# A masked cross-attention with layer norm: the order of all five engines' work written anew

## The chip, the cores and the metric

The kernel runs on one core of one Trainium2 chip. TensorE (PE in the profile) multiplies into PSUM, VectorE (DVE) and ScalarE (ACT) read PSUM and SBUF, GpSimd (POOL) works on SBUF alone, and SyncE (SP) only issues DMAs. Each engine takes its instructions strictly in the order in which the program lists them, and engines wait for each other by semaphores. The metric is the device time of the kernel in microseconds (us): before the change 507.44, the median of 3 runs (507.23 to 507.62).

## The reference

```python
qs  = (q @ wq).reshape(Bq, Lq, H, HD)        # q = x: 4 x 2048 rows of 512; H = 16 heads of HD = 32
ks_ = (k @ wk); vs = (v @ wv)                # k = v = context: 4 x 77 rows of 512
scores = einsum('bhqd,bhkd->bhqk', qs, ks_) / sqrt(HD)
scores = where(mask, -inf, scores)
attn = einsum('bhqk,bhkd->bhqd', softmax(scores), vs)
out  = attn @ wo + q
mu, var = mean(out), mean((out - mu) ** 2)   # over the 512 columns
return (out - mu) / sqrt(var + 1e-5) * gamma + beta
```

Everything is float32. The kernel multiplies the large matrices as a high and a low part (a float32 number rounded to the format `F32R`, and the rest), and adds three products: high by high, high by low, low by high.

## The kernel before, in words

The 8192 rows of x are cut into 64 tiles of 128 rows; two tiles are a block (32 blocks, numbered b), and four tiles are a group of 512 rows whose q is computed together (16 groups). The work is a list of small steps, one letter each, and the table `ORDER` writes out by hand in which order all of them are recorded. Since every engine works in the order of recording, the table sets each engine's order as well. No scheduler moves anything later. The steps that matter here:

- `Q` (`q_visit`, `q_rows`, matmuls on L275): one quarter of the heads' q for a group: 12 matmuls of 128x512, for each of 4 chunks of the contraction x high by wq high, x low by wq high, x high by wq low. `q` (`q_evac`, L289) copies the result from PSUM to SBUF on DVE.
- `S` (`scores`, L405): the scores of one tile, 64 small matmuls into four PSUM banks. `T` (`maxima`, L422) on DVE adds the mask and finds a row's greatest score, a quarter of the heads a step; `e` (`exps`, L437) on ACT exponentiates and sums; `r` (L447, DVE) takes the reciprocal, `n` (L452, POOL) multiplies by it.
- `t` (L473, DVE) transposes a tile in 32x32 squares into a buffer `B`, and 12 steps `P` (L484) per block are the DMAs that regroup it into `PT`, each by a queue that its last letter names: s for SP, a for ACT, g for POOL.
- `V` (`av`, L498): the product with the values for one block, 32 recorded matmuls. `a` (L527, ACT) rounds it to the high part `AH`, `b` (L531, DVE) makes the low part `AL`.
- `O` (`o_proj`, L554): the output projection of one tile, 12 matmuls of 128x512 into a bank `po`: for each chunk AH by wo high, AH by wo low, AL by wo high. `+` (L563, DVE) adds x, `s` (L577, L578, DVE) takes mean and variance, `v` (`rsqrt`, L583 to L586, four small operations on POOL) makes scale and shift for a block, `k` (`scale`, L592, ACT) applies them, `f` and `)` (L595, L598, POOL) multiply by gamma and add beta, `w` (SP) stores.
- `g` (`load_xT`) and `x` (`load_x`) are loads by SP; `i` (L265, ACT) and `j` (L269, POOL) make the high and low parts of x.

On PE there are so three kinds of stretches: wide matmuls (Q, O and, early, the values and keys), scores (S), and values' products (V). A second table, `SLOTS`, says which buffer each new tile takes; PSUM has 8 banks. `wait_for` adds a wait by hand: where DVE makes the low part of a weight out of two SBUF tiles (`F`, `G`), the next POOL step of the kinds j, n, f and `)` waits until that is done. The last eight tiles (`u`, `y`, `z`, `~` steps, the set `ALONE`) are normalised one by one by other functions.

Of the kernel before, what the change touches and what calls it, by code (L numbers as in the profile page):

```python
# [17 lines left out]
P = 128  # L18
# [16 lines left out]
for b in range(4):  # L35
# [7 lines left out]
NPB = 3  # L43
KSCALE = 1.0 / HD**0.5
# [7 lines left out]
F2 n1 e2.2 g6 T3.3 T3.0 T3.2 T2.1 j4 t1 P0.3s P0.2s P0.0s P0.5s e3.3 Q6 q6 G0 q7 B0 B2 e2.0 G3 G1 D0 e2.1 q5 e3.2 T3.1  # L52
P0.9s e2.3 r2 e3.1 e3.0 i6 G2 g7 P0.10s P0.11s S4 T4.3 e4.3 P0.7s T4.2 P0.8s i7 e4.2 B1 r3 Z1.s T4.0 e4.0 n2 T4.1 t2
Z0.s Q10 P0.4s n3 t3 P0.6s D2 P0.1s Z3.s S6 T6.2 T6.0 j6 D1 T6.3 P1.3s q10 T6.1 e4.1 r4 P1.0s P1.5s Q9 q9 e6.0 S5 T5.2
T5.0 e6.1 P1.2s P1.1s P1.8s j7 Q14 Z16.s P1.6s n4 t4 S7 Z2.s T7.3 e5.2 e6.3 e6.2 e7.3 T7.0 e7.0 T7.2 T5.3 T5.1 r6
P1.11s T7.1 e7.1 e7.2 q14 P1.10s P1.9s P1.7s P1.4s Q8 q8 Q11 q11 r7 Q13 n6 t6 e5.3 e5.1 e5.0 S9 T9.0 n7 T9.3 t7 r5 n5
V1 a1.1 a1.0 b1.0 x0 g8 i8 j8 g9 b1.1 T9.1 V0 a0.1 T9.2 Z8.s b0.1 x3 Z15.s O2 L1 i9 x2 S8 P3.6s P3.2s P3.8s j9 t5 e9.1
a0.0 b0.0 e9.2 e9.0 +2 T8.3 e8.3 T8.1 e8.1 =24.8 T8.0 e8.0 s2 T8.2 O3 +3 s3 q13 v1 P3.10s Z14.s P3.0s O0 P3.7s P3.9s
P3.1s Z4.s P3.5s e9.3 S10 T10.2 +0 Y1 Z13.s P3.4s x4 T10.3 e8.2 P3.11s P2.7s P2.8s P3.3s T10.1 e10.3 r9 k3 e10.1 T10.0
# [115 lines left out]
def xattn_layernorm(  # L175
# [84 lines left out]
    def load_xT(g, c):  # L260
        fx[g, c] = buf([P, 2, GRP], F32, "xtf", name=f"xtf_{g}_{c}")
        nc.sync.dma_start(fx[g, c], xT[g, :, c : c + 2])
# [538 lines left out]
```

## Time and profile before

| | us |
|---|---|
| median of 3 runs | 507.44 (507.23 to 507.62) |
| profiled execution, first to last instruction (span) | 506.2 |
| median less span | 1.24 |
| PE busy | 498.8 (99%) |
| ACT busy | 473.9 (94%) |
| DVE busy | 460.5 (91%) |
| POOL busy | 421.3 (83%) |

For the profiled execution the profile gives the span; the time of that execution as the runs measure it is not listed, so the span stands for it. Busy time is the union of an engine's instructions; an instruction's recorded length can overlap the next one's, since the engines are pipelined. The granted TensorE clock was 0.998 over the span.

### The profile page before, as it was taken

The numbers are of one execution on the slowest core, as the hardware profiler recorded it, in microseconds if no ns is written. First come the engines' busy times: TensorE is split into PE (matmuls) and PEld (weight loads), VectorE is DVE, ScalarE is ACT, GpSimd is POOL, SyncE is SP. The second block draws the span as 40 slices with busy tenths as digits, with TensorE's granted clock in tenths as the row PEclk, the third lists the DMA queues.
The fourth block names the chain that finished last, engine by engine and source line by source line (L and its number), as shares of the span: only waits on it lengthen the run. The fifth ranks groups of instructions, "written<-read, shape, count | busy, mean of one in ns | idle before, by whom it ended". The sixth has DMA issues, their size and how long they took to land.

```text
span 506.2 us, 20312 instructions
## 1 busy us (share of the span) xinstructions
PE 498.8 (99%) x6831; PEld 383.1 (76%) x6831; DVE 460.5 (91%) x2539; ACT 473.9 (94%) x2248; POOL 421.3 (83%) x387
## 2 busy tenths in 40 slices
PE   9999999999999999999999999999999999999995
PEld 6987778777777777777777777777777777877773
DVE  5799988999899999898898898998999999899997
ACT  6699999999999999999999999999999998999851
POOL 2666464789886798989989887999998999999896
PEclk9999999999999999999999999999999999999999
DMA  8957577889886796859887778877888769888746
GB/s 306 396 197 175 135 212 183 221 210 217 247 242 178 177 248 199 249 165 253 243 216 204 200 207 240 230 201 193 248 232 225 207 177 293 247 199 222 183 150 232
DMA packets 58782, 110.86 MB, mean 219 GB/s; under 512 B 9462, under 2 KB 11278, under 8 KB 58678
## 3 DMA queue, kind: packets, MB, share of 16 engines
q1 hardware_dynamic: 54502, 101.30, 71.1%
q0 software_dynamic: 2496, 5.77, 4.0%
q10 hardware_dynamic: 1680, 2.49, 2.0%
q8 instruction: 54, 0.88, 0.8%
q14 instruction: 50, 0.41, 0.3%
HBM read 41.79 MB, written 16.78 MB: 116 GB/s over the span
## 4 chain that ended last, share of the span: by engine, by line
PE 98%; DMA 1%; DVE 1%; ACT 0%; issue 0%; DVEq 0%
PE po L554 36%; PE pq L275 35%; PE pa L498 11%; PE sc L405 11%; PE pv L326 2%; PE pk L299 1%; PE pq L685 1%; DMA stage_a<-kin 1%; PE pa L513 0%; DVE xtl L637 0%; PE po L543 0%; DVE st L606 0%; DVE po L634 0%; ACT woh L672 0%; DVE mvt L608 0%
## 5 line engine op out<-in xcount | busy, mean ns | idle before, releaser
L437 ACT ACTIVATE pbuf<-pbuf,nm 128x77 f32<-128x77 f32 x1024 | 353.0, 358 | 5.2 <-DVE nm L422 3.6
L437 ACT ACTIVATION_READ_ACCUMULATOR pbuf<-pbuf,nm 128x1 f32 x1024 | 203.2, 198 | 0.0
L422 DVE CUSTOM_DVE_ANT_0 pbuf<-sc,mb 128x77 f32<-128x77 f32 x1024 | 169.7, 231 | 7.4 <-PE sc L405 5.8
L452 POOL TENSOR_TENSOR pbuf<-pbuf,ri 128x1232 f32<-128x1232 f32 x63 | 142.2, 2258 | 36.7 <-DVE ri L447 25.4
L554 PE MATMUL po<-woh,AH 128*128 128x512 f32 x256 | 103.5, 404 | 0.0
L473 DVE STREAM_TRANSPOSE B<-pbuf 128x1280 f32<-128x1280 f32 x64 | 96.1, 1502 | 5.8 <-POOL pbuf L452 2.4
L275 PE MATMUL pq<-xth,wqh 128*128 128x512 f32 (+1 forms) x256 | 100.8, 394 | 0.2
L554 PE MATMUL po<-wol,AH 128*128 128x512 f32 x256 | 99.9, 390 | 0.0
L554 PE MATMUL po<-woh,AL 128*128 128x512 f32 x256 | 99.8, 390 | 0.0
L275 PE MATMUL pq<-xth,wql 128*128 128x512 f32 (+1 forms) x256 | 98.1, 383 | 0.0
L275 PE MATMUL pq<-xtl,wqh 128*128 128x512 f32 (+1 forms) x256 | 98.1, 383 | 0.0
L422 DVE DVE_READ_ACCUMULATOR2_ANT nm<- 128x1 f32 x1024 | 84.4, 82 | 0.0
L598 POOL TENSOR_TENSOR o<-o,bet 128x512 f32<-128x512 f32 x56 | 72.1, 1291 | 1.8
L595 POOL TENSOR_TENSOR o<-o,gam 128x512 f32<-128x512 f32 x56 | 72.2, 1293 | 0.1
L269 POOL TENSOR_TENSOR xtl<-xtf,xth 128x1024 fp32r<-128x1024 f32 x28 | 67.2, 2404 | 3.9 <-ACT xth L265 3.2
L405 PEld LDWEIGHTS sc<-kct,q 32*64 32x64 f32 x4096 | 51.4, 130 | 22.6 <-issue 12.2
L405 PE MATMUL sc<-kct,q 32*64 32x77 f32 x4096 | 61.2, 238 | 0.0
L498 PE MATMUL pa<-PT,vsb 96*32 96x256 f32 x992 | 59.7, 382 | 0.0
L554 PEld LDWEIGHTS po<-woh,AH 128*128 128x128 f32 x256 | 48.0, 188 | 14.3 <-issue 2.5
L275 PEld LDWEIGHTS pq<-xth,wqh 128*128 128x128 f32 x256 | 48.1, 188 | 13.7 <-DVE nm L422 1.2
L554 PEld LDWEIGHTS po<-woh,AL 128*128 128x128 f32 x256 | 48.1, 188 | 10.5 <-DVE AL L531 0.2
L275 PEld LDWEIGHTS pq<-xth,wql 128*128 128x128 f32 x256 | 48.1, 188 | 9.7
(108 smaller groups left out, 638.6 us busy)
## 6 DMA issues: line engine op xcount, KB each, us to landing
PT<-B SPq DMA_DIRECT2D x330, 128.0 KB
xtf<-xT SPq DMA_DIRECT2D x28, 512.0 KB
o<-x SPq DMA_DIRECT2D x56, 256.0 KB
out<-o SPq DMA_DIRECT2D x56, 256.0 KB
PT<-B POOLq DMA_DIRECT2D x25, 128.0 KB, 4.0
PT<-B ACTq DMA_DIRECT2D x17, 128.0 KB
stage_a<-kin SPq DMA_DIRECT2D x4, 410.0 KB
xtf<-xT SPq DMA_DIRECT2D x4, 256.0 KB
```

The source lines that it names most:

```text
L269: return nc.gpsimd.tensor_tensor(l[:, c : c + 2], fx.pop((g, c)), xh[g][:, c : c + 2].bitcast(F32), ALU.subtract)
L275: nc.tensor.matmul(pq, w[:, c, m * P : (m + 1) * P], r[g][:, c, rs], start=(n == 0), stop=(n == 11))
L326: nc.tensor.matmul(pv[: rows.stop - rows.start], ctx_s[c][i][:, rows], v[c], start=(n == 0), stop=(n == 11))
L405: mm = nc.tensor.matmul(sc[j][r0 : r0 + SR, g * NK : (g + 1) * NK], qs[q, g, rs.start + r0 : rs.start + r0 + SR], kct[q, g, t // TPB, keys ...
L422: nc.vector.tensor_tensor_reduce(pb[:, h // 2, (h % 2) * NK : (h % 2 + 1) * NK], scs[t][j][:, g * NK : (g + 1) * NK], mb[:, t % TPB, keys_ ...
L437: nc.scalar.activation(pb[:, h // 2, (h % 2) * NK : (h % 2 + 1) * NK], pb[:, h // 2, (h % 2) * NK : (h % 2 + 1) * NK], AF.Exp, bias=nmax[t ...
L452: return nc.gpsimd.tensor_tensor(pv, pv, rv.to_broadcast((P, NP, 2, NK)), ALU.mult)
L473: nc.vector.transpose(bt.rearrange("p c q r -> p q c r"), pbuf[t % NPB].rearrange("p q (c r) -> p q c r", c=5),)
L498: nc.tensor.matmul(pas[b, g // 2][HD * j : HD * (j + 1), (g % 2) * BLK : (g % 2 + 1) * BLK], vsb[:, 2 * b // TPB, h % 2, HD * (h // 2) : H ...
L554: nc.tensor.matmul(pos[t], a[:, c, rs], w[:, c, :], start=(first and c == 0 and n == 0), stop=(c == NC_D - 1 and n == 2),)
L595: return nc.gpsimd.tensor_tensor(od[t], od[t], gam, ALU.mult)
L598: return nc.gpsimd.tensor_tensor(od[t], od[t], bet, ALU.add)
```

## The change

The table `ORDER` is replaced from its second line on, and `SLOTS` with it. Every step of before is there once, on the same operands, with these differences.

- **Kinds on PE.** Counted in the table from before and in the new one, the number of places where PE goes from one kind (wide, scores, values) to another falls from 151 to 135 (the description of the change counts 134). Stretches of wide visits fall from 58 to 45, runs of scores from 62 to 60 (S46 S47 and S60 S61 are new pairs), runs of values' products by one (V28 V29). A V is now followed at once by an S in 26 places (15 before), and by a wide visit in 3 (15 before).
- **Low parts last.** In Q and O the 8 matmuls with the high parts stand first, the 4 with the low part last.
- **Scaling on VectorE.** 37 of 56 tiles are scaled by DVE (`k….1`, a subtraction and multiplication with two per-row scalars) and 19 by ACT as before. Where both tiles of a block are, two of POOL's four small operations in `v` fall away. The next POOL step of the kinds j, n, f, `)` or v waits until the scaling is done.
- **q on ScalarE.** 28 of the 60 copies of q go from DVE to ACT.
- **Queues.** ACT's queue issues 101 of the regrouping DMAs (21 before; the description counts the 97 of whole blocks), POOL's 9 (31 before), SP's 286 (344 before). ACT's queue also issues 20 loads of x and 8 of x transposed. In all ACT issues 129 DMAs, 108 more than before.
- **Pauses in PE's queue.** A number behind an O or Q spreads that many NOPs among the visit's matmuls: 147 in all, 19 of them in 9 visits early in the kernel, the rest in 15 visits from O48 on.

```diff
-T1.1 Q4 T1.2 e0.3 F0 T1.3 I0 e1.2 r0 n0 S2 q4 e1.0 S3 T2.3 T2.0 Q7 N Y0 x1 Q5 i5 F1 e1.1 F3 R2 e1.3 j5 i4 t0 T2.2 r1
+T1.1 Q4.4 T1.2 e0.3 F0 T1.3 I0 e1.2 r0 n0 S2 q4 e1.0 S3 T2.3 T2.0 Q7.4 N Y0 x1 Q5 i5 F1 e1.1 F3 R2 e1.3 j5 i4 t0 T2.2
...
+def hi_then_lo(wh, wl, hi, lo):
+    return [(w, hi, c) for c in range(NC_D) for w in (wh, wl)] + [(wh, lo, c) for c in range(NC_D)]
...
+CENTRED = {int(w[1:].split(".")[0]) for w in ORDER.split() if w[0] == "k" and "." in w}
...
-        nc.sync.dma_start(fx[g, c], xT[g, :, c : c + 2])
+        (nc.scalar if by_scalar else nc.sync).dma_start(fx[g, c], xT[g, :, c : c + 2])
...
+    def pad(n, nops):
+        for _ in range((n + 1) * nops // 12 - n * nops // 12):
+            nc.tensor.nop(hint="pad")
...
-        for c in range(NC_D):
-            for w, r in ((wqh, xh), (wqh, xl), (wql, xh)):
-                nc.tensor.matmul(pq, w[:, c, m * P : (m + 1) * P], r[g][:, c, rs], start=(n == 0), stop=(n == 11))
-                n += 1
+        for w, r, c in hi_then_lo(wqh, wql, xh, xl):
+            nc.tensor.matmul(pq, w[:, c, m * P : (m + 1) * P], r[g][:, c, rs], start=(n == 0), stop=(n == 11))
+            pad(n, nops)
+            n += 1
...
-            nc.vector.tensor_copy(once(qd, g, [P, NG, GRP], F32, "q")[:, m, :], pq)
+            copy = nc.scalar.copy if by_scalar else nc.vector.tensor_copy
+            copy(once(qd, g, [P, NG, GRP], F32, "q")[:, m, :], pq)
...
-        nc.sync.dma_start(od[t], x[t * P : (t + 1) * P, :])
+        (nc.scalar if by_scalar else nc.sync).dma_start(od[t], x[t * P : (t + 1) * P, :])
...
+        for n, (w, a, c) in enumerate(hi_then_lo(woh, wol, ah, al)):
+            nc.tensor.matmul(pos[t], a[:, c, rs], w[:, c, :], start=(first and n == 0), stop=(n == 11))
+            pad(n, nops)
...
-        nc.gpsimd.tensor_tensor(rn[:, 1, :], mv[:, :, 0], rn[:, 0, :], ALU.mult)
-        nc.gpsimd.tensor_tensor(rn[:, 1, :], rn[:, 1, :], mneg, ALU.mult)
+        if not {2 * b, 2 * b + 1} <= CENTRED:
+            nc.gpsimd.tensor_tensor(rn[:, 1, :], mv[:, :, 0], rn[:, 0, :], ALU.mult)
+            nc.gpsimd.tensor_tensor(rn[:, 1, :], rn[:, 1, :], mneg, ALU.mult)
...
+        if t in CENTRED:
+            mean = mvs[t // 2][:, tt, 0:1]
+            return nc.vector.tensor_scalar(o, pos.pop(t, o), mean, rn[:, 0, tt : tt + 1], ALU.subtract, ALU.mult)
...
-            if op in "FG":
+            if op in "FG" or op == "k" and k and int(k) in CENTRED - IN_PSUM:
                 shared = ins
-            elif shared and op in "jnf)":
-                wait_for(ins, shared, "VectorE's pass over two tiles of SBUF is begun ahead of GpSimd's")
+            elif shared and op in "jnf)v":
+                wait_for(ins, shared, "VectorE's pass over both of its ports is begun ahead of GpSimd's")
```

In the changed kernel's file the steps stand some 15 lines lower (scores L420, values' product L513, maxima L437, exponentials L452, transposes L488, regroupings L499, scaling L607 on DVE and L608 on ACT).

**PE, around the values' product of block 2.** `sc` are score banks, `pa` the values' product, `pq` a bank of q; a number is a buffer's. Before:

```order
L405 MATMUL sc_2_1864<-kct,q_1140 64x77
L405 MATMUL sc_3_1865<-kct,q_1140 64x77
L498 MATMUL pa_0_1916<-PT_1538,vsb 32x256 x8
L498 MATMUL pa_1_1917<-PT_1538,vsb 32x256 x8
L275 MATMUL pq_3_1957<-xth_1281,wqh 128x512
L275 MATMUL pq_3_1957<-xtl_1283,wqh 128x512
L275 MATMUL pq_3_1957<-xth_1281,wql 128x512
```

And now:

```order
L420 MATMUL sc_2_1853<-kct,q_1155 64x77
L420 MATMUL sc_3_1854<-kct,q_1155 64x77
L513 MATMUL pa_0_1912<-PT_1416,vsb 32x256 x8
L513 MATMUL pa_1_1913<-PT_1416,vsb 32x256 x8
L420 MATMUL sc_0_1986<-kct,q_1155 64x77
L420 MATMUL sc_1_1987<-kct,q_1155 64x77
L420 MATMUL sc_2_1988<-kct,q_1155 64x77
```

The wide visits that stood between the values' product and the next tile's scores are gone from there; they stand together with others, ahead of and behind this place.

**PE, the end of a visit of q** (`xth` and `xtl` are the high and low parts of x, `wqh` and `wql` those of wq), now:

```order
L288 MATMUL pq_0_1823<-xth_1303,wqh 128x512
L288 MATMUL pq_0_1823<-xth_1303,wql 128x512
L288 MATMUL pq_0_1823<-xtl_1422,wqh 128x512 x4
L420 MATMUL sc_0_1851<-kct,q_1155 64x77
L420 MATMUL sc_1_1852<-kct,q_1155 64x77
```

Before, the low part came with the second matmul of a visit, as the first fence's last three rows show; now it comes with the ninth.

**ACT, some tiles after the first blocks.** Rows of `o` are scalings, `pbuf` exponentials (x4 is a quarter of the heads), `AH` a high part. Before:

```order
L527 CAST AH_2993<-pa_0_2975 128x512
L437 ACTIVATE pbuf_80,sum_3027<-pbuf_80,nm_2960 128x77 x4
L265 CAST xth_2833<-xtf_2_2653 128x1024
L437 ACTIVATE pbuf_82,sum_2907<-pbuf_82,nm_2801 128x77 x4
L592 ACTIVATE o_2862<-o_2862,rn_2915 128x512
L592 ACTIVATE o_2354<-o_2354,rn_2915 128x512
```

And now:

```order
L554 DMA o_3115<-x 128x512
L452 ACTIVATE pbuf_80,sum_3034<-pbuf_80,nm_3006 128x77 x8
L499 DMA PT_3085<-B_3003 32x2x512
L452 ACTIVATE pbuf_80,sum_3034<-pbuf_80,nm_3006 128x77 x4
L499 DMA PT_3085<-B_3003 32x2x512
L452 ACTIVATE pbuf_81,sum_3187<-pbuf_81,nm_3103 128x77 x4
L272 DMA xtf_2_3192<-xT 128x1024
```

Where two scalings stood among the exponentials, loads of x and regrouping DMAs now stand between their groups; before, no DMA stood on this queue ahead of block 23's.

More of the change, by code (lines that the diff above doesn't have):

```diff
@@ L55 @@
[L55 to L59, printed above, removed]
@@ L126 @@
-x48 e56.3 w45 e56.2 r56 v23 k46 P26.11s P26.10g T57.3 V25 P26.9a P26.2a w41 x57 x63 x53 e57.0 n55 t55 P27.5s S58
-P27.6s T58.2 a25.0 e57.3 e57.2 e57.1 n56 P27.9s P27.8g T58.0 a25.1 e58.0 f46 P27.1g )46 Q60 k47 P27.0s w46 x50 x60 q60
-b25.0 P27.11g r57 n57 T58.3 T58.1 e58.1 e58.2 t56 e58.3 Q62 S59 T59.3 s49 T59.1 T59.2 q62 P27.10g x62 e59.3 P27.4a O48
-+48 r58 s48 b25.1 f47 P27.3g T59.0 P27.2g t57 P27.7a Q61 q61 )47 w47 e59.2 Q63 q63 v24 k48 k49 V26 a26.0 b26.0 n58
-P28.4g x52 P28.0s S60 T60.3 T60.1 P28.10g x51 x55 P28.5s P28.1s T60.2 f49 P28.6g P28.3g P28.2g e59.0 e59.1 r59 n59 f48
@@ new lines @@
+S59 t56 x57.1 f47 s49 T59.2 r57 T59.1 e58.0 P27.9s v24 Q63.11 Q60.10 P27.11s e58.1 k49.1 a26.0 T59.3 e59.1 n57 T59.0
+x50.1 e59.0 b26.1 w45 x63.1 r58 t57 O50.19 q63.1 q60.1 P28.5s e59.3 b26.0 n58 e59.2 f49 S60 t58 k48.1 P28.11s P28.1s
++50 T60.0 e60.0 S61 P28.4s )49 T60.1 T60.2 )47 )46 w47 O51.13 r59 s50 w49 P28.8s P28.6s P28.9a T60.3 T61.1 T61.0 e60.1
+T61.3 n59 V27 P28.3a S62 +51 P28.0s e60.2 t59 x53 e60.3 O52.9 T61.2 f48 P28.10a s51 x52 P28.7s P28.2s T62.3 r60 T62.1
+e61.3 a27.1 O53.4 a27.0 x56 b27.1 v25 b27.0 x54.1 e61.2 P29.7a P29.9s P29.2s P29.0s e62.3 P29.11a e61.1 T62.2 +53
@@ L146 @@
+IN_PSUM = {int(w[1:].split(".")[0]) for w in ORDER.split() if w[0] == "k" and w.endswith(".2")}
 SLOTS = {
     "mm": (
[L148 to L151 removed]
@@ L153 @@
+        "1042673536741053265031472650314275065213764051430672156730"
     ),
@@ L156 @@
     "xtl": "10101010101010101",
-    "xtf": "010101010101010110101010101010",
-    "PT": "10100101010101010101010101010101011",
+    "xtf": "010101010101001000101010101011",
+    "PT": "1010010101010101010101010101010101",
     "B": "0101011010101010101010101010101010",
@@ L543, in resid, with o_proj @@
         nc.tensor.matmul(pos[t], ident, od[t], start=True, stop=False)
-    def o_proj(t):
+    def o_proj(t, nops=0):
         b, tt = divmod(t, 2)
@@ L551, in o_proj @@
             pos[t] = bank(f"po_{t}")
-        for c in range(NC_D):
-            for n, (a, w) in enumerate(((ah, woh), (ah, wol), (al, woh))):
-                nc.tensor.matmul(
-                    pos[t],
-                    a[:, c, rs],
-                    w[:, c, :],
-                    start=(first and c == 0 and n == 0),
-                    stop=(c == NC_D - 1 and n == 2),
-                )
+        for n, (w, a, c) in enumerate(hi_then_lo(woh, wol, ah, al)):
+            nc.tensor.matmul(pos[t], a[:, c, rs], w[:, c, :], start=(first and n == 0), stop=(n == 11))
+            pad(n, nops)
     def residual(t):
+        if t in IN_PSUM:
+            return residual_psum(t)
         nc.vector.tensor_tensor(od[t], pos.pop(t), od[t], ALU.add)
```

207 lines of the change are left out of this document (107 added, 100 removed).

## The prediction

> **What bounds the kernel now.** I read the page's busy shares and the chain that ended last first, then the busy time by stretch, then the chain in order of time.
>
> ```profile
> PE 498.8 (99%) x6831; PEld 383.1 (76%) x6831; DVE 460.5 (91%) x2539; ACT 473.9 (94%) x2248; POOL 421.3 (83%) x387
> PE 98%; DMA 1%; DVE 1%; ACT 0%; issue 0%; DVEq 0%
> 100.00:200.00 100.00, 100.00 (x1439) 76.32 (x1438) 93.17 (x564) 99.84 (x482) 84.41 (x68) 1.00 0.81 214
> 200.00:300.00 100.00, 100.00 (x1439) 76.46 (x1438) 90.83 (x508) 98.58 (x467) 91.03 (x79) 1.00 0.79 218
> 300.00:400.00 100.00, 99.99 (x1378) 76.01 (x1377) 92.38 (x532) 98.94 (x478) 92.94 (x79) 1.00 0.81 224
> ```
>
> The columns of the last three rows are PE, PEld, DVE, ACT, POOL, the granted clock and DMA. PE is without a pause, and 98% of the chain runs along it: the end comes earlier only if PE's own stream gets shorter. But ACT is busy 297 of 300 us, so a faster PE can be caught by ACT, and DVE has only 7.9 of 100 us free. What PE's stream costs is read from the chain in order of time (start, length, what):
>
> ```profile
> 20.93 1.74 PE sc L405 x101
> 68.74 3.59 PE pa L498 x64
> 93.89 0.88 PE sc L405 x57
> 94.78 2.98 PE pq L275 x12
> 97.76 2.72 PE po L554 x12
> 100.47 0.88 PE sc L405 x52
> 101.36 1.86 PE pa L498 x32
> 103.22 2.96 PE pq L275 x12
> 106.18 2.72 PE po L554 x12
> 108.90 0.88 PE sc L405 x52
> 109.78 5.68 PE pq L275 x24
> 118.21 2.96 PE po L554 x12
> 143.36 5.65 PE pq L275 x24
> ```
>
> A wide visit of 12 matmuls takes 2.72 us where another wide visit stands before it (97.76, 106.18). A whole stretch of them takes more: one alone 2.96 (118.21), two 5.68 (109.78), which is 5.44 and again 0.24. So every stretch of wide visits pays 0.24 us once, between 0.21 (5.65) and 0.26 (2.98, a first visit that another follows). Scores take 0.88 us after a values' product (93.89) and after wide visits (100.47) alike, a values' product 1.86 us; the cost of leaving them is in these lengths.
>
> **The change part by part.** *Fewer kinds.* Stretches of wide visits go from 58 to 45: 13 x 0.24 = 3.1 us less, 2.7 to 3.4 by the two ends. Putting V next to S instead of next to wide visits costs nothing of itself, since neither length depends on its neighbour. The new pair of values' products saves 2 x 1.86 - 3.59 = 0.13 us, the two new pairs of scores 2 x 0.88 - 1.74 = 0.02 each: together 0.2.
>
> *Low parts last.* The low part is needed eight matmuls later, 8 x 0.227 = 1.8 us. Where PE was kept by it, this shows at the last visits but one:
>
> ```profile
> 493.98 0.80 PE L554 MATMUL po<-woh,AH 128*128 128x512 f32 x1
> 494.00 0.68 DVE L531 TENSOR_TENSOR AL<-pa,AH 128x512 fp32r<-128x512 f32 x1
> 494.62 0.40 PE L554 MATMUL po<-wol,AH 128*128 128x512 f32 x1
> 494.73 0.19 PEld L554 LDWEIGHTS po<-woh,AL 128*128 128x128 f32 x1 [0.15 <-DVE AL L531]
> ```
>
> From the first to the second matmul are 0.64 us instead of 2.72 / 12 = 0.227, while DVE makes AL and PE's queue stands at it: 0.4 us that the new order hides behind eight matmuls. Elsewhere the first visit's surplus varies between 0.21 and 0.26; if a late low part is what makes it long, 45 stretches x at most 0.02 give 0 to 0.9, and I take 0.4.
>
> *NOPs.* No NOP is in this trace. The nearest thing that only PE's sequencer executes is the semaphore wait:
>
> ```profile
> L405 PEldq EVENT_SEMAPHORE  x143: 51/51/872, 47.0 to 463.1; - x143
> ```
>
> 143 of them at 51 ns lie beside matmuls, in a PE without pauses. So a NOP costs between nothing and 0.051 us, 147 of them 0 to 7.5 us. I take nothing: even 25 in one visit are 1.3 us of sequencer inside 2.72 us of matmuls.
>
> *ACT.* It loses 37 scalings and gains 28 copies of q, whose nearest row on ACT is the rounding of a PSUM bank:
>
> ```profile
> L592 ACT ACTIVATE o<-o,rn 128x512 f32<-128x512 f32 x56 | 44.2, 817 | 1.5 <-POOL mvt L619 1.2 <-POOL rn L586 0.3
> L527 ACT CAST AH<-pa 128x512 fp32r<-128x512 f32 x64 | 35.8, 580 | 4.5 <-PE pa L498 2.9 <-PE pa L513 0.7 <-ACT pbuf L437 0.4
> L289 DVE COPY q<-pq 128x512 f32<-128x512 f32 x60 | 40.0, 674 | 5.7 <-PE pq L275 5.7
> L385 DVE TENSOR_SCALAR mb<-m 128x1536 bf16<-128x1536 uint8 x1 | 1.0, 952 | 0.0
> ```
>
> That is -30.2 + 16.2 = -14.0 us. Against it stand 108 more DMA issues on its queue:
>
> ```profile
> 387.79 0.61 ACTq L484 DMA_DIRECT2D PT<-B  x1
> 388.44 1.05 ACT L265 CAST xth<-xtf 128x1024 fp32r<-128x1024 f32 x1 [0.55 <-DMA PT<-B]
> 391.58 0.59 ACTq L484 DMA_DIRECT2D PT<-B  x1
> 391.71 0.19 ACT L437 ACTIVATION_READ_ACCUMULATOR pbuf<-pbuf,nm 128x1 f32 x1
> 391.81 0.35 ACT L437 ACTIVATE pbuf<-pbuf,nm 128x77 f32<-128x77 f32 x1
> 392.22 0.61 ACTq L484 DMA_DIRECT2D PT<-B  x1
> ```
>
> An issue occupies ACT's sequencer for 0.6 us. At 391.58 and 392.22 the engine went on with exponentials that were already queued: no cost. At 387.79 its queue held nothing, and the next cast began 0.55 us late. So an issue costs 0 to 0.61, in all 0 to 66 us; I take 0.05, or 5 us, because most new ones stand among exponentials, and one that follows a full queue is covered. PE's shorter stream asks ACT for 4 us less in 500, so 10 of the 14 us may go to DMAs before ACT sets the pace: 0.09 each.
>
> *DVE* loses 28 x 0.674 = 18.9 us and gains 37 scalings. There is no scaling of an SBUF tile in the trace; a third of the 1536 columns of L385 is 0.32 us, the copy of 512 columns from PSUM 0.67: 12 to 25 us more. I take 0.4 each, since source and target are SBUF as with L385's; DVE's sum falls by 4. [...]
>
> *POOL* loses 22 issues and, in the 14 blocks with both tiles moved, 28 small operations, and its scalings' inputs now come from DVE:
>
> ```profile
> L484 POOL DMA_DIRECT2D PT<-B x31 | 17.5, 565 | 2.4 <-DMA PT<-B 1.4 <-issue 0.9
> L585 POOL TENSOR_TENSOR rn<-mv,rn 128x2 f32<-128x2 f32 x28 | 5.5, 195 | 2.2
> ```
>
> 22 x 0.565 + 28 x 0.195 = 18 us less, in 421. Its new waits (a step behind each scaling) come out of that and of its 10 us in 100 that are free. SP issues 86 DMAs fewer; on the 108 that ACT takes over, ACT's next exponentials queue behind any wait for a transpose, and DVE's normal order behind those.
>
> *The sum*, against the profiled execution: 506.2 - 3.1 - 0.2 - 0.4 - 0.4, and 0.4 for new waits of PE on engines that follow more closely (between 0 and the rivals' 7), is 502.5. The median lies 1.24 above that span (507.44), so **503.7 us**.
>
> **The rivals.** *More than that:* every stretch pays 0.21, nothing waits: 506.2 - 13 x 0.24 - 45 x 0.03 - 0.2 - 0.4 = 501.1, or 502.4 by the runs' measure. For it speaks that the surplus reached 0.21 in places, against it that ACT has no slack to spare.
>
> *The gain is caught by ACT:* at 0.13 per issue ACT's sum is as before, 14.0 against -14.0, and it was at 99% beside a PE at 100%: the end stays at about 507. Of the issues quoted, one in three was exposed. Above 0.13 the time grows by 1.08 us per 0.01; at 0.16 it is 507.4 + 3.2 = 510.7. Against it: an ACT that lags has a full queue, and a full queue covers an issue.
>
> *DVE and POOL shut each other out (slower).* A DVE operation on two SBUF tiles begins while POOL works:
>
> ```profile
> 37.57 2.41 POOL L269 TENSOR_TENSOR xtl<-xtf,xth 128x1024 fp32r<-128x1024 f32 x1
> 39.67 0.85 DVE L367 TENSOR_TENSOR wol<-stage_b,woh 128x512 fp32r<-128x512 f32 x1
> 41.05 1.28 DVE L367 TENSOR_TENSOR wol<-stage_b,woh 128x512 fp32r<-128x512 f32 x2
> L452 POOL TENSOR_TENSOR pbuf<-pbuf,ri 128x1232 f32<-128x1232 f32 x63 | 142.2, 2258 | 36.7 <-DVE ri L447 25.4 <-DVE nm L422 5.3 <-DVE wol L367 5.0
> L595 POOL TENSOR_TENSOR o<-o,gam 128x512 f32<-128x512 f32 x56 | 72.2, 1293 | 0.1
> ```
>
> The first took 0.85 us with 0.31 us of POOL's operation beside it, the other two 0.64 each with POOL idle. If a scaling behaves so, it waits for the rest of POOL's operation: half of 1.3 to 2.4 us, 0.9 on average, times 37 = 33 us, against 38 us that DVE has free (7.9 of 100, over 480) plus the 4 of relief. So it decides from about 1.1 us per tile; at 1.3, with each scaling behind most of an operation, 48 - 42 = 6 us late: 503.7 + 6 = 510. For it speaks POOL at 90% busy; against it that scalings mostly stand behind a step `v` of their own block, where POOL has just finished, and the step after them is held back by hand. [...]
>
> *The change doesn't do what it says:* the count of kinds is in the order itself, so the wide stretches are 45; only if a pause of PE inside a stretch cost the same 0.24 again would it bring nothing. No pause in this trace shows that.
>
> **How the numbers follow.** Less than 0.2% (1.0 us) can't be told from no change in this kernel. My forecast, 502.6 to 505.5, has 0.55; more gain 0.07; a part of the gain eaten, 505.5 to 506.4, 0.10; caught by ACT, 506.4 to 508.4, 0.12; ACT above 0.13 per issue 0.08; DVE and POOL 0.08. That makes faster 0.72, same 0.12, slower 0.16. The range, 501.5 to 509.0, leaves out most of the two slow rivals and little of the fast one.
>
> **What would show it.** In the new profile PE's chain should still hold 97% or more; a wide stretch should read 2.72 n + 0.24 or a little less, and 45 of them. ACT's busy time falls to about 460, DVE's to 455, POOL's to 403. If ACT's DMAs are exposed, ACT shows idle time before casts and exponentials "<-DMA PT<-B" or "issue", of 5 us or more; if the lock decides, the scaling's mean (L607) is over 1 us, and PEld waits "<-DVE nm" grow beyond their few us. The forecast is wrong if PE shows pauses of over 2 us in all, or if the values' product and scores next to each other are longer than 1.86 and 0.88.

## The result, and the profile after it

The changed kernel takes **535.26 us** (median of 4 runs, 532.33 to 536.30); the kernel before, run beside it, 507.34 us (507.08 to 507.62). The ratio is 1.054, with a 95% interval from 1.052 to 1.056: 28 us slower, where 3.7 us less were forecast. The profiled run took 534.35 us, its span 532.5. In the last experiment below one execution of four fell into a state with a lower granted clock (0.982, against 0.992 and 0.993 in the others) and is left out of its median.

The busy shares and the chain that ended last, of the changed kernel:

```profile
PE 506.8 (95%) x6831; PEld 390.0 (73%) x6831; DVE 460.8 (87%) x2548; ACT 463.7 (87%) x2239; POOL 404.3 (76%) x337
PE 32%; DMA 17%; DVE 15%; POOL 11%; ACT 10%; SPq 7%; issue 5%; ACTq 1%; POOLq 0%; DVEq 0%
```

The busy times of ACT, DVE and POOL came out near the forecast's (about 460, 455 and 403 us). What did not is the chain: 98% of it ran along PE before, 32% do now. PE waits, and no engine is full: ACT is idle for 13% of the span where it was idle for 6%. By matmul starts in the trace, 18 visits take over 0.45 us more than their usual length (2.72, 0.88 or 1.86 us, and 0.24 for the first of a wide stretch), 25.9 us in all; before there was no such visit.

Who waits for what is read from the groups of instructions (busy us, mean ns, then the idle time of the engine just before them and what ended it). First ACT's exponentials and high parts and DVE's scalings, of the changed kernel:

```profile
L452 ACT ACTIVATE pbuf<-pbuf,nm 128x77 f32<-128x77 f32 x1024 | 353.1, 354 | 33.8 <-issue 7.6 <-DMA PT<-B 6.3 <-DVE nm L437 5.4
L542 ACT CAST AH<-pa 128x512 fp32r<-128x512 f32 x64 | 35.8, 577 | 9.1 <-DMA PT<-B 4.9 <-issue 2.2 <-DVE st L622 1.2
L607 DVE TENSOR_SCALAR o<-o,mv,rn 128x512 f32<-128x512 f32 x37 | 20.0, 552 | 0.8 <-POOL rn L595 0.7
```

and the exponentials of the kernel before:

```profile
L437 ACT ACTIVATE pbuf<-pbuf,nm 128x77 f32<-128x77 f32 x1024 | 353.0, 358 | 5.2 <-DVE nm L422 3.6 <-DMA PT<-B 1.5
```

The exponentials take what they took (353 us), but ACT stands still for 33.8 us ahead of them instead of 5.2, and the releasers named first are ACT's own sequencer and a regrouping DMA (together 13.9 us; DVE's maxima and low parts and other DMAs share most of the rest). The forecast had set down this very sign, "ACT shows idle time before casts and exponentials `<-DMA PT<-B` or `issue`, of 5 us or more", for the case that ACT's DMAs are exposed. The sign for the lock, as the forecast calls the rival in which DVE and POOL shut each other out, a scaling of over 1 us, is absent: 0.552 us.

One of the places in the changed kernel, in ACT's timeline (start us, us, instruction, idle before), with SP's queue at the same time:

```profile
87.25 0.85 ACT L398 ACTIVATE mb<-m 128x768 bf16<-128x768 uint8 x1
92.34 0.59 ACTq L499 DMA_DIRECT2D PT<-B  x1
92.98 0.36 ACT L452 ACTIVATE pbuf<-pbuf,nm 128x77 f32<-128x77 f32 x1 [4.88 <-DMA PT<-B]
...
84.34 0.55 SPq L272 DMA_DIRECT2D xtf<-xT  x1
84.93 1.90 SPq L499 DMA_DIRECT2D PT<-B  x2
86.93 0.53 SPq L554 DMA_DIRECT2D o<-x  x1
87.51 1.22 SPq L499 DMA_DIRECT2D PT<-B  x2
```

and the chain of waits that ends there:

```profile
87.51 4.81 DMA PT<-B
92.32 0.02 issue
92.34 0.59 ACTq L499
92.93 0.05 issue
92.98 1.39 ACT pbuf L452 x7
...
95.83 0.35 ACT q L304
```

ACT has finished at 88.10 and its next instruction is a regrouping DMA. That DMA issues only at 92.34, when *another* regrouping, which SP issued at 87.51, has landed. Nothing in the data ties the two together. In the built program every DMA of SP's and ACT's queues reports its end on one of eight semaphores, given out strictly in turn over all 588 DMAs (459 of SP, 129 of ACT), and the program has a DMA wait until the one that used its semaphore eight DMAs earlier has landed, whichever queue that stood on. Of ACT's 129 DMAs, 122 have such a wait (84 in the DMA itself, 38 in a wait just ahead of it), and 95 of these are for a DMA of SP's queue. It binds the other way too: 101 of SP's DMAs wait for one of ACT's. Behind the DMA stand the exponentials, behind them the copy of q at 95.73, and PE waits for that copy:

```profile
96.35 1.59 PE L420 MATMUL sc<-kct,q 32*64 32x77 f32 x64 [2.25 <-ACT q L304]
98.68 0.77 PE L288 MATMUL pq<-xth,wqh 128*128 128x512 f32 x1 [0.74 <-DVE nm L437]
99.25 0.63 PE L288 MATMUL pq<-xth,wql 128*128 128x512 f32 x1
99.67 0.63 PE L288 MATMUL pq<-xth,wqh 128*128 128x512 f32 x1
100.10 0.63 PE L288 MATMUL pq<-xth,wql 128*128 128x512 f32 x1
```

From 99.25 on a wide matmul starts every 0.427 us instead of every 0.227. Busy time by stretch, with the granted clock as the third number from the end, says why:

```profile
85.00:92.00 7.00, 7.00 (x92) 5.64 (x91) 3.41 (x20) 3.10 (x15) 4.72 (x4) 1.00 0.93 256
92.00:97.00 5.00, 2.75 (x87) 1.66 (x77) 3.99 (x20) 4.02 (x22) 0.00 (x0) 0.89 0.77 208
97.00:103.00 6.00, 5.26 (x64) 4.14 (x52) 4.60 (x51) 6.00 (x25) 4.32 (x2) 0.52 0.54 141
103.00:110.00 7.00, 7.00 (x95) 5.57 (x97) 5.17 (x12) 7.00 (x41) 5.97 (x6) 1.00 0.58 176
```

PE was busy for 2.75 of 5 us, and in the 6 us after that it was granted 0.52 of its clock. The granted clock is 0.50 in four stretches of this trace while PE has work: 95.9 to 102.7, 126.6 to 130.0, 406.5 to 409.9 and 495.3 to 498.6 us. In the first three lie 21 wide matmuls of 0.20 us too much each, 4.2 of the 25.9 us. The longest step between two matmul starts before such a stretch was 2.6 us. What sets the clock is not shown by these runs; that it fell after pauses of PE is.

### The profile page after: what moved, and what is told of

Read it like the earlier page. It is cut to its first block, busy times and chain, and to the rows that moved or that the text cites. A ratio compares the mean times of both kernels' runs of the same rounds, so it can differ in the third digit from the quotient of the medians.

```text
span 532.5 us, 20420 instructions
## 1 busy us (share of the span) xinstructions
PE 506.8 (95%) x6831; PEld 390.0 (73%) x6831; DVE 460.8 (87%) x2548; ACT 463.7 (87%) x2239; POOL 404.3 (76%) x337
## 4 chain that ended last, share of the span: by engine, by line
PE 32%; DMA 17%; DVE 15%; POOL 11%; ACT 10%; SPq 7%; issue 5%; ACTq 1%; POOLq 0%; DVEq 0%
PE pq L288 13%; DMA PT<-B 11%; PE po L568 9%; ACT pbuf L452 8%; SPq L499 5%; DVE B L488 4%; POOL pbuf L467 4%; PE sc L420 4%; DVE pbuf L437 3%; PE pa L513 3%; DMA out<-o 3%; POOL o L614 2%; POOL xtl L279 2%; PE pv L341 2%; POOL o L611 1%
## 5 line engine op out<-in xcount | busy, mean ns | idle before, releaser
L452 ACT ACTIVATE pbuf<-pbuf,nm 128x77 f32<-128x77 f32 x1024 | 353.1, 354 | 33.8 <-issue 7.6
L452 ACT ACTIVATION_READ_ACCUMULATOR pbuf<-pbuf,nm 128x1 f32 x1024 | 198.5, 194 | 0.0
L437 DVE CUSTOM_DVE_ANT_0 pbuf<-sc,mb 128x77 f32<-128x77 f32 x1024 | 171.0, 232 | 8.6 <-PE sc L420 6.3
L568 PE MATMUL po<-woh,AH 128*128 128x512 f32 x256 | 105.4, 412 | 3.6 <-DVE AL L546 2.4
L488 DVE STREAM_TRANSPOSE B<-pbuf 128x1280 f32<-128x1280 f32 x64 | 96.0, 1501 | 12.8 <-DMA PT<-B 6.4
L568 PE MATMUL po<-wol,AH 128*128 128x512 f32 x256 | 101.9, 398 | 0.0
L437 DVE DVE_READ_ACCUMULATOR2_ANT nm<- 128x1 f32 x1024 | 84.7, 83 | 0.0
L420 PEld LDWEIGHTS sc<-kct,q 32*64 32x64 f32 x4096 | 53.6, 131 | 31.1 <-issue 13.9
L420 PE MATMUL sc<-kct,q 32*64 32x77 f32 x4096 | 64.1, 239 | 7.4 <-ACT q L304 4.9
L568 PE MATMUL po<-woh,AL 128*128 128x512 f32 x256 | 68.9, 390 | 2.1 <-DVE AL L546 2.1
L288 PE MATMUL pq<-xtl,wqh 128*128 128x512 f32 (+1 forms) x256 | 67.0, 383 | 0.0
L513 PE MATMUL pa<-PT,vsb 96*32 96x256 f32 x992 | 61.1, 387 | 2.7 <-DVE o L574 2.5
L568 PEld LDWEIGHTS po<-woh,AL 128*128 128x128 f32 x256 | 48.3, 189 | 12.7 <-DVE AL L546 2.5
L568 PEld LDWEIGHTS po<-wol,AH 128*128 128x128 f32 x256 | 49.4, 193 | 9.7 <-issue 0.2
```

What stands on the lines that cost most here:

```text
L288: nc.tensor.matmul(pq, w[:, c, m * P : (m + 1) * P], r[g][:, c, rs], start=(n == 0), stop=(n == 11))
L420: mm = nc.tensor.matmul(sc[j][r0 : r0 + SR, g * NK : (g + 1) * NK], qs[q, g, rs.start + r0 : rs.start + r0 + SR], kct[q, g, t // TPB, keys ...
L437: nc.vector.tensor_tensor_reduce(pb[:, h // 2, (h % 2) * NK : (h % 2 + 1) * NK], scs[t][j][:, g * NK : (g + 1) * NK], mb[:, t % TPB, keys_ ...
L452: nc.scalar.activation(pb[:, h // 2, (h % 2) * NK : (h % 2 + 1) * NK], pb[:, h // 2, (h % 2) * NK : (h % 2 + 1) * NK], AF.Exp, bias=nmax[t ...
L488: nc.vector.transpose(bt.rearrange("p c q r -> p q c r"), pbuf[t % NPB].rearrange("p q (c r) -> p q c r", c=5),)
L513: nc.tensor.matmul(pas[b, g // 2][HD * j : HD * (j + 1), (g % 2) * BLK : (g % 2 + 1) * BLK], vsb[:, 2 * b // TPB, h % 2, HD * (h // 2) : H ...
```

## The experiments

Theory A is what this place suggests: ACT pays for its DMAs with stops, and PE pays for ACT's. The rivals are the scalings with POOL and their hand-made waits (B), and the new order itself, however the work is spread over engines and queues (C, D). Letters are used as the expectations use them.

### Each part alone

**All DMAs back on SP's queue.** Every word of the order that ends on ACT's queue is moved to SP's, in place:

```diff
-P3.9a ... g11.1 ... x3.1
+P3.9s ... g11   ... x3
```

> The changed kernel with every DMA that ACT's queue issues (101 regroupings, 20 loads of x, 8 of x transposed) issued by SP's queue again, at the same place of the table. Theory A (ACT stands still behind its own DMAs, each of which waits for an earlier DMA of another queue): ACT's idle time between 60 and 500 us falls from some 45 us to under 15, PE's stalls go with it, and the time is 502 to 509. Rival B (scaling on VectorE and GpSimd shut each other out): at least half of the loss stays, 520 or more. Rival C (the new order of PE itself starves it): likewise 520 or more, with PE waiting for VectorE or PSUM.

Measured: 530.35 us (529.71 to 533.42), ratio 1.046 [1.042, 1.050]. Only 5 us come back, and ACT's idle time between 60 and 500 us is still 35.4 us (40.9 in the change, 11.9 before), although no DMA stands on its queue: idle time of ACT alone does not prove theory A. As the sole cause theory A seemed to fall here.

**Only the 28 loads back on SP's queue** (`g11.1` to `g11`, `x3.1` to `x3`).

> The changed kernel with only the 28 loads (x and x transposed) back on SP's queue; the 101 regroupings stay on ACT's. Theory A, if each DMA of ACT's queue is as likely to stand: 28 of 129 less, so about a fifth of the 28 us is won back, 526 to 532; if the loads alone do the harm, under 512; if they do none, 533 to 537.

Measured: 540.83 us (539.65 to 542.00), ratio 1.065: slower than the change by 5.6 us, and outside every range set down. The loads on ACT's queue are no cost but a gain.

**The kernel before, with the same 97 regroupings on ACT's queue** (`P3.9s` to `P3.9a` and so on; 86 come from SP's queue, 7 from POOL's, and 4 were on ACT's already), nothing else changed.

> The kernel before with one part of the change alone: the 97 regroupings that the change gives to ACT's queue are issued by ACT's queue at the place where they stood in the old table. Theory A: ACT stands still behind them, idle time of 20 us or more, and the kernel is slower by 2 to 8%, 517 to 548. Rivals B and C: ACT's queue is harmless, 505 to 510.

Measured: 538.74 us (536.90 to 540.59), ratio 1.060. Moving these DMAs costs 31 us in the old order, by itself.

**The kernel before, with the low parts last** (`hi_then_lo` in both visits), nothing else changed.

> The kernel before with only the order of the matmuls within a visit of q and of the output projection changed: high parts first, low parts last. From the prediction's term: 0.4 us less at the last visits and 0 to 0.9 elsewhere, 506.0 to 507.0. If the order within a visit is indifferent: 507.3.

Measured: 507.32 us, ratio 0.9993 [0.998, 1.001]: no difference that can be measured, where 0.8 us less had been put into the forecast's sum. The interval reaches from 1.1 us less to 0.5 us more, so the times alone do not exclude the 0.8.

**The new order alone**: all DMAs on SP's queue, the scalings back on ACT (`k7.1` to `k7`), the copies of q back on DVE (`q17.1` to `q17`).

> The changed kernel with every DMA of ScalarE's queue back on SyncE's, the 37 scalings back on ScalarE and the 28 copies of q back on VectorE: only the new order (and low parts last, NOPs) is left. With the DMAs on SyncE alone the run before this one took 530.35 us. Theory D (the new order issues the regroupings too late: in the two orders the last regrouping of a block stands 10.6 us of TensorE work ahead of its values' product before, 6.0 us in the change, on the mean of blocks 2 to 29): nothing comes back, 525 to 533. Theory B (the scalings on VectorE hold GpSimd and shut it out): 503 to 510. Both in part: 511 to 524.

Measured: 539.53 us (538.03 to 541.03), ratio 1.062. Slower than with the scalings and copies moved (530.35): in the new order they belong where the change put them. SP's queue holds 387 regroupings here, 43 more than in the kernel before (344), so a part of this loss can be that queue's; the new order with the old queues was not tried.

**The change of engines alone**, in the old order: the 37 scalings on DVE, the 28 copies on ACT (`k7` to `k7.1`, `q17` to `q17.1`).

> The kernel before in its own order, with the same 37 scalings on VectorE and the same 28 copies of q on ScalarE as the change (low parts last too, which alone measured 507.3): the change of engines alone. Theory B (scalings and GpSimd): 515 or more. Theory D (place of the regroupings) and theory A (ScalarE's queue): 503 to 511, since ScalarE is relieved by 14 us and VectorE's sum hardly changes; 505 to 508 if TensorE stays without pauses.

Measured: 549.01 us (547.99 to 552.45), ratio 1.083, the largest loss of all. The scaling's row in this run and its row in the change above differ by 0.3 us a tile:

```profile
L606 DVE TENSOR_SCALAR o<-o,mv,rn 128x512 f32<-128x512 f32 x37 | 31.4, 859 | 4.0 <-POOL rn L594 4.0
```

0.859 us each against 0.552. Moved into an order that was not made for them, the scalings are slower, although the hand-made waits are in this kernel too. That fits theory B, by which they meet POOL's operations, for this kernel; how the 41 us divide between the scalings and the copies of q was not tried.

So the parts don't add: 31 us, 32 us and 41 us each alone, 28 us together. Each of these three mixtures loses more than the whole change, and these six runs can't say which part costs the 28. The next ones leave the change as it is and take one suspect out.

### Regroupings issued earlier

In the order before, the last regrouping of a block stands 10.6 us of PE's work ahead of its values' product (mean of blocks 2 to 29, from the order and 2.72, 0.88 and 1.86 us per visit); in the change 6.0, at four blocks under 1. Theory D took that for the cause. Each `P` word is recorded up to 5 us of PE's work earlier, once with all DMAs on SP, once on the change's own queues:

```diff
-=24.8 n13 Z11.s P5.11s g14.1
+P5.11s ... =24.8 n13 Z11.s g14.1
```

> The changed kernel with every DMA on SyncE's queue (530.35 us) and each regrouping recorded up to 5 us of TensorE work earlier, never ahead of its block's second transpose: the last one then stands 9.0 us ahead of the values' product on the mean instead of 6.0. No other engine's order changes (GpSimd's few regroupings aside). Theory D: most of the loss goes, 505 to 518. Theory B, or an order of the engines that is bad in itself: 525 to 533. SyncE too full for any place of them: 525 or more, with TensorE still waiting behind a chain of SyncE issues.

> The changed kernel as it is (101 regroupings and the 28 loads' share on ScalarE's queue, 535.26 us) with each regrouping recorded up to 5 us of TensorE work earlier, as in the run before. Theory D: 512 to 526. Theory A (each of ScalarE's DMAs costs ScalarE its issue and a wait for earlier DMAs or transposes wherever it stands): 530 to 545, ScalarE's idle time as large as now (55.8 us).

Measured: 546.62 us (542.60 to 550.64) on SP and 549.37 us (547.71 to 551.04) on the change's queues: 16 and 14 us *slower* than the same kernels with the late places. Theory D falls. On SP's queue the traces show why: ahead of regroupings the queue waits 72.8 us for DVE's transposes, against 47.7 with the late places, with everything that stands behind it.

### One suspect out

**Without the 97 regroupings on ACT's queue.**

```diff
-P3.9a P3.1a P2.7a ...
+
```

> The changed kernel without the 97 regroupings that the change gave to ScalarE's queue (from block 2 on): they are left out, so the values' product reads what an earlier block left there, and the output is not the reference's. Every other instruction of every engine stands as in the change; the two PT buffers are held for the whole run instead of taken anew for each block. Some 12.7 of 111 MB of transfers go too. Theory A (what ScalarE's DMAs cost ScalarE: 0.59 us of issue and a wait for earlier DMAs each) as the main cause in the change: 503 to 513. If the new order or the scalings cost as much by themselves (orders alone measured 530 to 549): 522 or more.

Measured: **511.01 us** (510.56 to 512.80), ratio 1.007 [1.005, 1.010]: 24.3 of the 27.9 us are gone. In the profile of this run:

```profile
PE 497.9 (98%) x6831; PEld 384.6 (76%) x6831; DVE 460.3 (90%) x2548; ACT 463.4 (91%) x2239; POOL 403.9 (79%) x337
PE 88%; DVE 5%; DMA 3%; issue 2%; POOL 1%; SPq 1%; POOLq 0%; ACT 0%; DVEq 0%
L447 ACT ACTIVATE pbuf<-pbuf,nm 128x77 f32<-128x77 f32 x1024 | 353.1, 354 | 8.7 <-DVE nm L432 6.8 <-POOL pbuf L474 1.6
```

The chain runs along PE again, and ACT's idle time ahead of the exponentials is back at 8.7 us (33.8 with them, 5.2 before). ACT's idle time over the whole run, summed over the gaps in its timeline, is 33.9 us, against 57.6 in the change: 23.7 us less for 24.3 us of time. After the first 4 us no matmul runs at half clock: the granted clock of the page is 9 tenths or more in 39 of its 40 slices of 12.7 us, and 7 in the last, where a matmul still starts every 0.23 us (499.34 to 500.03).

**Without the 37 scalings.**

> The changed kernel without the 37 scalings on VectorE (left out: 37 output tiles are not normalised), and so without the waits that hold a GpSimd step behind each. Theory B (scalings, their waits and GpSimd) as the main cause: 503 to 515. Theory A: 528 or more, since VectorE loses 20 of 461 us and ScalarE's stops stay. Half the loss back, 515 to 528, if the two lengthen one loop together.

Measured: 535.42 us (533.97 to 537.82), ratio 1.055: nothing comes back, although DVE has 17 us less to do. Theory B falls for the change itself.

**Without either.**

> The changed kernel without the 97 regroupings and without the 37 scalings (both left out as in the two runs before). If those two carry the loss: 502 to 508, TensorE without pauses of over half a microsecond, which also gives the size of the change's own gain on TensorE (forecast: 3.7 us). If the new order is bad in itself: 520 or more.

Measured: 511.70 us (510.59 to 512.63), ratio 1.008: as without the regroupings alone, and above the 502 to 508 that was expected. PE still has three visits that are over 1 us too long, so the gain of 3.7 us on PE does not show here either.

**Without the hand-made waits behind the scalings.**

```diff
-            if op in "FG" or op == "k" and k and int(k) in CENTRED - IN_PSUM:
+            if op in "FG":
```

> The changed kernel without the hand-made waits that hold GpSimd's next step until a scaling on VectorE has begun (nothing is left out; only the order of starting between the two engines is free). Theory B by these waits (GpSimd waited 10.4 us for the scalings before the gain, 11 us in one place before a split): 520 to 530. Theory B by the shared port (each scaling then stands behind GpSimd's operations): slower, 540 to 560, with a scaling of over 1 us. Neither: 532 to 538.

Measured: 547.89 us (542.10 to 550.70), ratio 1.075: 12.6 us slower.

```profile
L607 DVE TENSOR_SCALAR o<-o,mv,rn 128x512 f32<-128x512 f32 x37 | 36.1, 988 | 1.1 <-POOL rn L595 1.1
```

The scaling goes from 0.552 to 0.988 us on the mean. In this run's trace 25 of the 37 take 0.45 to 0.57 us, as in the change; the other 12 take 1.2 to 4.1 us, and each of these ends 0.28 to 0.30 us after an operation of POOL that ran beside it. So in these 12 places a scaling ended only once POOL's operation had, and 0.28 to 0.30 us after it. POOL does shut DVE out there, as the prediction feared, and in this order the waits that the change brings along keep most of that away (with them two of the 37 take over 0.9 us, 0.91 and 0.95). What the two engines share, a port or something else, is not shown by this run.

### What the regroupings cost ACT by

Leaving them out takes away four things at once: ACT's issues, its waits, the bytes, and the values' product's dependence. Moving them to SP had kept the last two and gave back little, so theory E, that the product waits for late regroupings whoever issues them, was still open.

**Transfers of one number in their place**, same queue, same places, same waits, to a buffer that nothing reads:

```diff
+        if queue is nc.scalar and b < 31:
+            nc.scalar.dma_start(spare[32 * k : 32 * k + 32, 0, :1], bts[b][32 * i : 32 * i + 32, c, :1])
+            return
```

> The changed kernel in which each of the 97 regroupings on ScalarE's queue carries only one number of each of 32 partitions, from the same place of the same transposed block to a buffer that nothing reads (so the regrouping itself is left out, and the output is not the reference's). ScalarE issues as many transfers as in the change and waits for the same transposes and earlier transfers; the values' product does not wait for them, and their 12.7 MB are gone. Without them at all the run before measured 511.0, with them 535.3. Theory A (ScalarE standing still for issue and waits): 528 to 537. Theory E (the values' product waits for regroupings that land late, or transfers crowd each other, whoever issues them; the run with all on SyncE, 530.4, speaks for it): 509 to 515.

Measured: 533.70 us (531.34 to 534.27), ratio 1.049 [1.046, 1.052]. The bytes and the product's dependence are worth some 1.6 us, which these runs can't tell from nothing; 22.7 us come from ACT having 97 DMAs in its queue at these places (the kernel of 511.01 us holds the PT buffers in the same way). SP's queue could be held by them too, through the shared semaphores, but in this trace no DMA of SP's waits for one of them. Theory A stands, theory E falls for the change.

**The number taken from a constant**, so that no transpose is waited for:

```diff
-            nc.scalar.dma_start(spare[32 * k : 32 * k + 32, 0, :1], bts[b][32 * i : 32 * i + 32, c, :1])
+            nc.scalar.dma_start(spare[32 * k : 32 * k + 32, 0, :1], gam[32 * i : 32 * i + 32, :1])
```

> As the run before, but the number comes from a constant, so that the transfer waits for no transpose: what is left is the issue on ScalarE (0.59 us x 97 = 57 us beside or between 464 us of work) and the wait for the earlier transfer on the same completion semaphore. If it takes as long as the run before, the wait for transposes costs nothing; if 511, the wait for transposes is what ScalarE pays in theory A; between them it parts the two.

Measured: 527.11 us (526.68 to 531.45), ratio 1.039 [1.034, 1.044]. The wait for transposes is worth 6.6 us; 16.1 us remain although these transfers depend on nothing. ACT still stops for them, as the same place shows in this run's timeline of SP and ACT:

```profile
87.23 1.23 SPq L511 DMA_DIRECT2D PT<-B  x2
...
86.93 0.85 ACT L400 ACTIVATE mb<-m 128x768 bf16<-128x768 uint8 x1
92.67 0.51 ACTq L507 DMA_DIRECT2D spare<-gam  x1
93.24 0.36 ACT L454 ACTIVATE pbuf<-pbuf,nm 128x77 f32<-128x77 f32 x1 [5.46 <-DMA PT<-B]
```

ACT is free at 87.78, and the transfer from a constant issues at 92.67, when the regrouping that SP issued at 87.23 has landed.

**The regroupings on POOL's queue** (`P3.9a` to `P3.9g`).

> The changed kernel with the 97 regroupings on GpSimd's queue instead of ScalarE's (nothing left out; the 0.57 us that such an issue keeps GpSimd busy make 55 us beside its 404). Theory A: 511 to 525, since GpSimd is the least busy engine, though its steps after the scalings and the normalisations come later. Theory E: 528 or more, since the regroupings stand at the same late places.

Measured: 540.98 us (540.29 to 541.67), ratio 1.064: no better. With all DMAs on SP's queue (530.35 us) that makes three queues that can't carry them in this order. What each makes late is in one row, DVE's transposes, for the change, SP's queue and POOL's queue, in this order:

```profile
L488 DVE STREAM_TRANSPOSE B<-pbuf 128x1280 f32<-128x1280 f32 x64 | 96.0, 1501 | 12.8 <-DMA PT<-B 6.4 <-POOL pbuf L467 4.0 <-POOL o L614 1.4
```

```profile
L488 DVE STREAM_TRANSPOSE B<-pbuf 128x1280 f32<-128x1280 f32 x64 | 96.0, 1501 | 28.3 <-DMA PT<-B 23.0 <-POOL pbuf L467 3.2 <-issue 1.3
```

```profile
L488 DVE STREAM_TRANSPOSE B<-pbuf 128x1280 f32<-128x1280 f32 x64 | 96.1, 1503 | 33.8 <-POOL pbuf L467 21.6 <-DMA PT<-B 6.4 <-issue 5.2
```

On ACT the exponentials are late (33.8 us, above). On SP the regroupings themselves are: the next block's transposes wait 23.0 us for them to leave the buffer. On POOL the normalisations are, and the transposes wait 21.6 us for these. The loss is of similar size each time and has another name. That these rows carry the 23 and 33 us of the two runs is read from the traces, not tried.

### What is left

**Other semaphores.** The builder's model of time, which decides which DMA gets which of the eight, is turned off; every engine's order stays.

```diff
-    with tile.TileContext(nc, schedule_with_timeline_sim=True) as tc:
+    with tile.TileContext(nc, schedule_with_timeline_sim=False) as tc:
```

> The changed kernel, nothing left out, every engine's and queue's instructions in the same order; only the numbering of the eight semaphores by which transfers report their end is laid out anew (by the program's builder, without its model of time), so that a transfer waits for another earlier transfer than in the change. By the issue times in the changed kernel's trace, 6 of ScalarE's 129 transfers would now wait for one that SyncE issues later than they stood there, and 45 for one issued less than 5 us ahead (37 in the change). Theory A by waits for earlier transfers: the time moves, 538 to 560. If these waits are not the cause (ScalarE's stops come from the issue alone or from the transposes): 533 to 537.

Measured: 535.23 us (532.55 to 537.21), ratio 1.054: the same as the change. The forecast of 538 to 560 was wrong. But ACT's stops are not the same ones: in the change ACT waits over 0.3 us between its last instruction and a DMA's issue at 12 places, 24.6 us in all, and at 88 it is SP's regrouping of 87.51 that holds it; here it is 16 places, 17.0 us, and the place at 88 is gone, while one at 156 is new. The stops follow the numbering; the time does not change with it. PE still loses at the first place, 1.65 us at the scores of 94.8 us: the chain there now runs over two of DVE's transposes (91.22 to 93.70), which waited 3.7 us for regroupings to leave their buffer. Here another engine stands right behind ACT's stop, so a stop taken away is not a stop won. So how the 16.1 us divide between the issues (10.8 us of ACT's idle time in the change lie under an issue) and the waits for earlier DMAs stays open.

**VectorE's order at the very end.** In the change DVE's last step for tile 62 stands ahead of the moments of tile 63, and these begin at 526.75, some 1.7 us after the last matmul; before they began at once (500.07).

```diff
-z62 ... O63 s63
+... O63 s63 z62
```

> The changed kernel without the 97 regroupings (left out, 511.01 us) in which VectorE's last step for tile 62 stands behind the moments of tile 63 instead of ahead of them. In the change's trace the moments of the last tile begin 2.0 us after the last matmul, in the kernel before at once: 1.0 to 2.0 us less, 509.0 to 510.0. If the end waits for something else, 511.

Measured: 512.09 us (509.86 to 513.93), ratio 1.008 [1.004, 1.011]: no difference from 511.01 that these runs can tell. By the traces the stretch from the last matmul to the end went from 7.9 to 7.4 us; before it was 6.2.

**The loads back on SP's queue as well.**

> As the run before, and the 28 loads of x and xT that the change gave to ScalarE's queue are back on SyncE's. ScalarE then issues only the few regroupings of the last block. If the rest of the gap to the forecast of 503.7 is ScalarE's loads: 503 to 506. If it is the new order itself (late regroupings on SyncE's queue, scores that wait): 508 or more.

Measured: 515.09 us (513.23 to 516.92), ratio 1.014 [1.010, 1.018]: 3 us slower than 512.09, hardly clear of the scatter but the same way as with the loads alone on SP's queue (5.6 us). ACT's loads are not what keeps the kernel above the forecast. No mixture tried here was faster than the kernel before.

## Why the prediction was wrong

**The step that failed** is the price of ACT's DMAs: "an issue costs 0 to 0.61, in all 0 to 66 us; I take 0.05, or 5 us, because most new ones stand among exponentials, and one that follows a full queue is covered." The regroupings alone measured 24.3 us, 0.25 each. Three things were wrong in it.

*The bound counted the issue and left out the wait ahead of it.* The rows of before that the price was taken from had ACT's few DMAs from 370 us on. In the change's trace, the groups of that line on ACT's queue (min/median/max ns) are

```profile
L499 ACTq DMA_DIRECT2D PT<-B x101: 592/593/1072, 78.2 to 510.6; - x101
L499 ACTq EVENT_SEMAPHORE  x57: 17/38/4866, 78.0 to 508.3; - x57
```

The issue is the 0.6 us that was expected, and mostly covered as expected (10.8 us of 74 fell into idle time). What was not in the sum is the wait, for a transpose or for a DMA of another queue: up to 4.9 us at once. Without the wait for transposes the kernel was 6.6 us faster; how the other 16.1 us divide between the issues and the waits for earlier DMAs stays open. The prediction named the first kind ("ACT's next exponentials queue behind any wait for a transpose") and gave it no price; it did not look for the second, though which DMA waits for which stood in the program.

*Slack was taken as a sum.* "10 of the 14 us may go to DMAs before ACT sets the pace" treats relief spread over 500 us as if it could pay for a stop of 4 us at one place. ACT was idle for 13% of the changed kernel, and PE waited for it. The covering queue that the argument relied on ("an ACT that lags has a full queue") was empty at such a place: at 88.10 the DMA stood first.

*The stops had a price beyond their length.* After four of PE's pauses (1.9 to 2.4 us of idle time each) the granted clock was 0.50: 4.2 us at wide matmuls alone.

**The rival "caught by ACT"** had the right mechanism and too small a chance (0.08 above 0.13 per issue). Its own slope, 1.08 us per 0.01, gives 520 at the measured 0.25, not 535: it still counted ACT's relief against the stops. **DVE and POOL shutting each other out** decided nothing in the change, where the waits set by hand mostly prevent it: 0.552 us per scaling against the 0.4 taken, 5.6 us more for the 37, so DVE's busy time came out at 460.8 us (455 forecast; the prediction's own sum gives 456.4). But the 1.1 us from which it was to decide was too high: without the waits 0.988 us cost 12.6 us.

**Point by point, what held.** *Fewer kinds:* by the matmuls' starts, changes of kind went from 150 to 134 (the 151 and 135 of the count are runs of one kind) and stretches of wide visits from 58 to 45. Their median surplus after 25 us is 0.24 us before and 0.23 now, so the 3.1 us were there. Without the regroupings on ACT's queue the surplus of these stretches is 11.0 us against 12.7 before, 1.7 less instead of 3.0, so 1.3 us are new stalls, and 3.0 us more are lost at scores that wait: the gain is eaten before it reaches the end. *Scores and values' products* keep 0.88 and 1.86 us next to each other. *NOPs* cost nothing that shows: the visit with 25 of them takes 2.72 us (500.76 to 503.48), as one without.

*Low parts last* was wrong in the first of its two terms of 0.4 us; the second is too small for these runs. The step of 0.64 us at the last visits but one is still there, though the low part now comes with the ninth matmul only (seven matmuls later in a Q and six in an O, not eight):

```profile
518.98 0.80 PE L568 MATMUL po<-woh,AH 128*128 128x512 f32 x1
519.62 0.39 PE L568 MATMUL po<-wol,AH 128*128 128x512 f32 x1
```

DVE's low part ended near PE's next start in the trace of before, and I took the nearness for a cause; what makes this step is not known. *The end* was left out: 1.3 us more from the last matmul to the last instruction. The order of DVE's last rows differs there, but putting it back won nothing that these runs can tell.

**Against the forecast,** then: of the 31.6 us between 503.7 and 535.3, the regroupings on ACT's queue are 24.3. The other 7.3, read from the trace of the run without these, are no single step: the end (1.7 us in that run), the low parts (up to 0.8), stalls at scores and wide visits (4.3, of which 0.4 was forecast), and 0.8 because that run's median lies 2.0 us above its span and not 1.24. What makes those scores wait was not tried apart.

## What to carry to other kernels

In this kernel a DMA on ACT's queue cost ACT the wait (up to 4.9 us) as well as the issue (0.593 us): before moving one, look up in the built program what it waits for, its data and the earlier DMA whose semaphore it reuses, and when these will be done at that place. With PE without a pause and the other engines at 83 to 94%, the slack of an engine was not a sum to spend from: one stop of ACT of 4.2 us (88.10 to 92.34) went through to PE, which stood still for 2.25 us behind it, while 17 us of work taken off DVE changed nothing. To find what a change of many parts costs, take suspects out of the changed kernel; trying its parts one by one in mixtures with the old one gave 31, 32 and 41 us for parts of a whole of 28.

## What was not expected of the hardware

- PE's clock halved (0.50 granted over 6.8 us once and some 3.4 us three times, 0.427 us per wide matmul) after steps between matmul starts of 2.6 us and less; with the other semaphores a step of 3.4 us at 307 us was followed by no such stretch, nor was one of 2.5 us at 203 us in the change. In the 3.4 us ahead of each of the four stretches (as long as three of these are) PE was busy for 1.3 to 1.6 us; so it was from 201.7 to 205.1 us (1.63), with a granted clock of 1.00 behind it. By these the length of a pause alone does not decide it, and what does is not shown.
- An ACT DMA whose data depend on nothing stood still for 4.9 us, from 87.78 to 92.67, for a DMA of SP's queue (the number taken from a constant), by the program's semaphores.
- A float32 scaling of 128x512 from SBUF to SBUF took 0.552 us on DVE in the change's order with POOL held back, 0.988 us without that, and 0.859 us in the old order although POOL was held back there too.
